# A decoder layer whose planner weighs its streams by a table over time

## The chip, the cores and the metric

One core of one Trainium2 chip runs the kernel. The metric is device time in microseconds (us) of one execution; lower is better. Instruction engines are named as the profile names them: PE (tensor engine; PEld is its weight loads), DVE (vector), ACT (scalar), POOL (GpSimd) and SP (which only issues DMAs here).

## The reference

Four sequences of 1024 rows with 256 features pass one decoder layer. Cut to what matters:

```python
x = x + self_attention(layernorm(x))      # 16 heads of 16; causal; scores mix two products
x = x + cross_attention(layernorm(x), ctx, mask)   # 77 context rows, 16 heads of 16
x = x + ffn(layernorm(x))                 # 256 -> 768 -> 256

# self-attention: Q, K, V = x Wq^T + bq, ...; g = sigmoid(gate), by head
scores = (g * (Q W_cross) K^T + (1 - g) * Q K_mixed^T) / sqrt(16)
out = softmax(causal(scores)) V Wo^T + bo
# feedforward, with int32 weights divided by 127
out = (silu(x Wg^T) * (x Wu^T)) Wd^T
```

All arithmetic is to float32 accuracy.

## The kernel before, in words

**Work and tiles.** The 4096 rows are eight chunks of 512 rows (four sequences, `b`, of two halves, `n`). For each chunk there are five kinds of work. `project` (L975) normalizes the rows and makes keys, queries and values; each key and query block is split into a rounded part `hi` and a rest `lo` (`spread`, L919), which DMAs on SP's queue lay out by heads, since score matmuls use both parts. `maxima` (L1035) computes the scores once and reduces them on DVE to the largest per query (`mt`). `attend` (L1101) computes scores again with keys on the partitions, subtracts the maxima by another matmul (`sel`, `ms`), takes the exponential on ACT (`es`), and multiplies by the values. `cross_attention` (L1254) does the like for the 77 context rows. `ffn` (L1392) has six blocks of 128 hidden features: a gate and an up matmul group of four matmuls each (`wgT`, `wuT`, by `xh` and `xl`), a tanh on ACT (`h`), two products on DVE, then a rounding on ACT and a rest on POOL (`hT`); after two blocks come the down matmuls (`wdT`, `hT`).

**Streams and pieces.** Each kind of work is a stream: a Python generator that yields pieces, `piece(pe, use, at, ...)` (L565). A piece is one stretch of tensor work with the work on other engines that follows it: its estimated PE time, a list of engines with estimated times, the time from which its inputs are there, and the buffers that it takes (PSUM banks as `pair` or `single`, and slots such as `es`, `f2`, `w4`). The streams stand in the order maxima, cross-attention, attention, projection of the first half, projection of the second half, four streams that load weights (one for the cross-attention, three for the feedforward), feedforward. `mode` names how a piece uses the PE array: `rows` (64 rows of it, scores), `cols` (32 columns, values) or `whole`.

**The planner.** `weave` (L645) keeps an account of time while the program is built; nothing of it runs on the chip. At each step it asks for every stream when its next piece could start: inputs there, buffers free, PE free, 0.11 more for a change of mode, and no earlier than its first following engine can take it within a margin. To this time it adds the stream's lateness, `s.lates[s.chunk]` (L669), one number for each stream and chunk from the table `LATES` (L1499). The first stream in order that lies within 0.01 of the smallest sum goes next. The lateness counts in the choice only; the piece is booked at its own time. So a positive number makes a stream yield to others, a negative one puts it ahead. The planner then books PE, engines and buffers, and `perform` (L618) issues the recorded instructions in the order of the planned times, subject to the data they share. Each engine runs its own queue in that order.

**Fillers.** Where the account foresees that PE would idle over 1.3 us (`REST`, L683) while a bank is free, the planner issues matmuls that compute nothing that is used (`selB` by `sel`, `stirred`, L140), (idle - 0.7) / 0.235 of them.

All instructions that the planner issues are recorded under line 643, so the profile tells them apart by tile.

Of the kernel before, what the change touches and what calls it, by code (L numbers as in the profile page):

```python
# [27 lines left out]
def tile_decoder_layer(  # L28
# [68 lines left out]
    class Later:  # L97
        def __init__(self, make, where, steps=()):
            self.make, self.where, self.steps = make, where, steps
# [50 lines left out]
    def single():  # L150
        b = home("single", 8)
        return stirred(banks[:, b, :], banks[:, b, :])
# [163 lines left out]
    for name, sgn in (("cm_qk", 1), ("cm_kq", -1)):  # L316
        t = masks_f[name] = stage.tile([P, P], BF16, name=name + "f")
# [78 lines left out]
    t = single()  # L396
# [3 lines left out]
    for ec in range(NC):  # L400
        t = single()
# [8 lines left out]
    t = single()  # L410
# [10 lines left out]
    t = single()  # L421
# [42 lines left out]
    class Slots:  # L464
# [13 lines left out]
        def give(self, k, when):  # L478
            self.free[k] = when
# [31 lines left out]
    }  # L511
    LATE = 0.2
    SWITCH = 0.11
    WAIT = 0.01

    class Engine:
# [30 lines left out]
    class Stream:  # L547
        def __init__(self, make, lates=()):
            self.lates = lates
            self.chunk = -1  # L550
            self.got = {}
            self.fresh = {}
            self.end = self.done = 0.0
            self.pieces = make(self)
            self.next = next(self.pieces, None)
# [36 lines left out]
    def file(t, spans):  # L592

        last, at = 0, t
        for call in said:
            when = t
            if call[0] != "PE":
                of = [m for m in range(last, len(spans)) if spans[m][0] == call[0]]
                if of:
                    last = of[0]  # L600
                    _, when, at = spans[last]
                else:
                    when = at
            filed.append((when, *call))
        said.clear()
# [39 lines left out]
    def weave(*streams):  # L645
        while True:
            live = [s for s in streams if s.next is not None]
            if not live:
                assert not any(v for s in streams for v in s.fresh.values())
                return  # L650
            can = []
            for s in live:
                p = s.next
                if p["cond"] is not None and not p["cond"]():
                    continue
                t = max(p["at"], *(slots[k].when(c) for k, c in p["take"].items()), 0.0)
                if p["pe"]:

                    if p["mode"] != tensor["mode"]:
                        t = max(t, tensor["end"]) + SWITCH  # L660
                    else:
                        t = max(t + SWITCH, tensor["end"])
                t = max(t, tensor["end"])
                if p["use"] and p["take"]:

                    eng, us = p["use"][0]
                    t = max(t, busy[eng].start(t + p["pe"], us) - p["pe"] - 1.0)
                if t < 1.0e8:
                    can.append((t + (s.lates[s.chunk] if s.lates else 0.0), t, s))  # L669
            assert can, [s.next for s in live]  # L670
            soon = min(c[0] for c in can) + WAIT
            _, t, s = next(c for c in can if c[0] <= soon)
            p = s.next
            s.got = {k: [slots[k].take() for _ in range(c)] for k, c in p["take"].items()}
            for k, tokens in s.got.items():
                s.fresh.setdefault(k, []).extend(i for _, i in tokens)
            s.end = t + p["pe"]
            if p["pe"]:
                idle = t - tensor["end"]
                early = max([slots[k].when(1) for k in ("pair", "single") if k in p["take"]] or [t])  # L680
                if idle > REST and early < tensor["end"] + 0.5 and "selections" in flags:
                    stand["us"] = idle - 0.7
                elif idle > REST:  # L683
                    tensor["slow"] = t + COLD
                s.end += min(max(tensor["slow"] - t, 0.0) / 2, p["pe"])
                tensor.update(end=s.end, mode=p["mode"])
            for token in p["free"]:
                give(token, s.end)
            s.done = s.end
            spans = []  # L690
            for eng, us in p["use"]:
                s.done = busy[eng].run(s.done + LATE, us)
                spans.append((eng, s.done - us, s.done))
            hand["fresh"] = s.fresh
            s.next = next(s.pieces, None)
            hand["fresh"] = None
            file(t, spans)
# [788 lines left out]
    def every(part, lates, chunks=range(NQ)):  # L1486


        def pieces(st):
            for b in range(B):  # L1490
                for n in chunks:
                    st.chunk += 1
                    yield from part(st, b, n)

        return Stream(pieces, lates)
# [8 lines left out]
        [0.1069, 0.1944, 0.3468, 0.0000],  # L1504
        [0.0000, 0.0000, -0.5736, 0.0000, 0.0000, 0.4883, 0.5315, -4.4614],
    )
    streams = [
        every(maxima, LATES[0]), every(cross_attention, LATES[1]), every(attend, LATES[2]),
        *(every(project, LATES[3 + n], [n]) for n in range(NQ)),
        Stream(late_weights), *(Stream(lambda st, m=m: load_ffn(st, m)) for m in range(3)),  # L1510
        every(ffn, LATES[5]),
    ]
    weave(*streams)
    nc = core
    with tc.manual_schedule():
# [6 lines left out]
    t = single()  # L1522
# [53 lines left out]
```

## Time and profile before

| | |
|---|---|
| time, median of 3 runs | 1180.34 us (1180.18 to 1180.37) |
| the profiled execution | 1180.69 us |
| its span in the profile | 1178.1 us |
| mean granted clock of PE | 0.985 |
| DMA | 76.48 MB, 65 GB/s in the mean |
| filler matmuls | 112 |
| maxima's reductions on DVE | 384, 350.9 us |
| exponentials on ACT | 448, 360.2 us |

The span is the time from the first to the last instruction that the profile shows; the rest of the execution's time lies around it. The page gives each engine's busy time and its share of the span, then the chain of work that ended last, then groups of equal instructions: line, engine, operation, output<-input with tile names, shapes, the count, busy time in all, the mean duration of one in ns, and the idle time of the engine just ahead of them with what ended it. A list of waits has the engine and tile that waited, for whom, us in total, times, and the longest. A timeline has start, duration, engine, line, operation, and in brackets the idle time ahead. In a table of stretches each engine has its busy us and in parentheses its instructions; PEclk is the granted share of PE's clock.

### The profile page before, as it was taken

The numbers are of one execution on the slowest core, as the hardware profiler recorded it, in microseconds if no ns is written. First come the engines' busy times: TensorE is split into PE (matmuls) and PEld (weight loads), VectorE is DVE, ScalarE is ACT, GpSimd is POOL, SyncE is SP. The second block draws the span as 40 slices with busy tenths as digits, with TensorE's granted clock in tenths as the row PEclk, the third lists the DMA queues.
The fourth block names the chain that finished last, engine by engine and source line by source line (L and its number), as shares of the span: only waits on it lengthen the run. The fifth ranks groups of instructions, "written<-read, shape, count | busy, mean of one in ns | idle before, by whom it ended". The sixth has DMA issues, their size and how long they took to land.

```text
span 1178.1 us, 22519 instructions
## 1 busy us (share of the span) xinstructions
PE 1108.0 (94%) x9171; PEld 686.8 (58%) x9171; DVE 734.2 (62%) x1287; ACT 558.4 (47%) x785; POOL 131.9 (11%) x138
## 2 busy tenths in 40 slices
PE   5899999999899999999999999999998999999996
PEld 3555545566665565565655557555665555557675
DVE  5578855356588679445668768354689577127444
ACT  3153476554335545744444453675334555862422
POOL 4000100010110010021000011011200000012112
PEclk9799999999899999999999999999999999999999
DMA  6981315639430451125682251034953314004100
GB/s 125 138 133 42 95 27 100 84 57 141 57 72 2 70 72 37 37 33 96 97 119 50 46 70 33 1 99 66 135 83 51 51 25 84 2 1 77 31 36 21
DMA packets 65440, 76.48 MB, mean 65 GB/s; under 512 B 22450, under 2 KB 39398, under 8 KB 65331
## 3 DMA queue, kind: packets, MB, share of 16 engines
q1 hardware_dynamic: 64227, 74.62, 38.8%
q8 instruction: 74, 1.21, 0.5%
q10 hardware_dynamic: 1104, 0.35, 0.1%
q14 instruction: 35, 0.29, 0.1%
HBM read 15.28 MB, written 9.33 MB: 21 GB/s over the span
## 4 chain that ended last, share of the span: by engine, by line
PE 74%; DVE 10%; ACT 6%; DMA 6%; issue 2%; POOL 1%; SPq 1%; ACTq 0%; DVEq 0%; POOLq 0%
PE banks L643 74%; DVE mt L643 5%; ACT es L643 3%; DMA k<-lo 2%; DMA q<-lo 2%; DVE h L643 2%; POOL hT L643 1%; SPq L643 1%; ACT h L643 1%; DMA out_dram<-x 1%; DVE mx L643 1%; ACT hT L643 1%; DMA wk_n<-in_L_attn_Wk_dram 1%; DVE st L643 0%; DVE x L643 0%
## 5 line engine op out<-in xcount | busy, mean ns | idle before, releaser
L643 ACT ACTIVATE es<-banks 128x1024 f32<-128x1024 f32 (+3 forms) x448 | 360.2, 841 | 259.7 <-PE banks L643 235.2
L643 DVE TENSOR_REDUCE mt<-banks 128x2 f32<-128x1024 f32 (+3 forms) x384 | 350.9, 955 | 109.2 <-PE banks L643 105.6
L643 PE MATMUL banks<-k,q 64*128 64x512 f32 (+3 forms) x768 | 160.7, 423 | 17.0 <-DVE mt L643 6.8
L643 PE MATMUL banks<-q,k 64*128 64x512 f32 (+3 forms) x768 | 159.7, 411 | 9.7 <-ACT es L643 3.3
L643 PE MATMUL banks<-es,vs 128*32 128x512 f32 (+3 forms) x1536 | 163.7, 499 | 1.2 <-ACT es L643 0.6
L643 PEld LDWEIGHTS banks<-k,q 64*128 64x128 f32 x768 | 74.4, 187 | 102.3 <-ACT es L643 35.5
L643 PE MATMUL banks<-ms,sel 64*128 64x512 f32 (+3 forms) x768 | 133.6, 343 | 0.1
L643 PEld LDWEIGHTS banks<-q,k 64*128 64x128 f32 x768 | 72.9, 185 | 97.3 <-ACT es L643 50.8
L643 POOL TENSOR_TENSOR hT<-h,hT 128x512 fp32r<-128x512 f32 x48 | 61.6, 1284 | 332.9 <-ACT hT L643 332.9
L643 PEld LDWEIGHTS <-id 64*128 64x128 bf16 x2048 | 61.0, 96 | 51.6 <-issue 38.1
L643 PEld LDWEIGHTS banks<-ms,sel 64*128 64x128 f32 x768 | 73.6, 187 | 3.8 <-DVE ms L643 0.5
L643 DVE SCALAR_TENSOR_TENSOR h<-h,banks 128x512 f32<-128x512 f32 x48 | 33.0, 687 | 65.8 <-ACT h L643 65.2
L643 POOL TENSOR_TENSOR rs<-ve,mhalf 128x4 f32<-128x4 f32 x23 | 24.3, 1059 | 408.7 <-DVE ve L643 408.7
L643 PE MATMUL banks<-cm_qk,id 64*128 64x128 bf16 (+1 forms) x1024 | 68.1, 211 | 0.0
L643 PE MATMUL banks<-cm_kq,id 64*128 64x64 bf16 (+1 forms) x1024 | 66.8, 208 | 0.0
L643 ACT ACTIVATE h<-banks 128x512 f32<-128x512 f32 x48 | 28.7, 597 | 62.6 <-PE banks L643 58.1
L643 PE MATMUL banks<-wdT,hT 128*128 128x256 f32 x384 | 55.6, 294 | 1.3 <-POOL hT L643 0.7
L643 DVE TENSOR_REDUCE mx<-banks 128x8 f32<-128x616 f32 x64 | 47.8, 793 | 12.7 <-PE banks L643 12.7
L643 PEld LDWEIGHTS banks<-es,vs 128*32 128x32 f32 x1536 | 31.8, 108 | 40.8 <-issue 26.1
L643 PEld LDWEIGHTS banks<-wdT,hT 128*128 128x128 f32 x384 | 49.9, 194 | 7.4 <-DVE x L643 1.7
L643 ACT CAST hT<-h 128x512 fp32r<-128x512 f32 x48 | 29.7, 619 | 50.2 <-DVE h L643 50.2
L643 ACT COPY xnT<-banks 128x1024 f32<-128x1024 f32 x31 | 31.3, 1014 | 45.1 <-PE banks L643 45.1
(185 smaller groups left out, 1569.2 us busy)
## 6 DMA issues: line engine op xcount, KB each, us to landing
q<-hi SPq DMA_DIRECT2D x128, 128.0 KB, 5.0
q<-lo SPq DMA_DIRECT2D x128, 128.0 KB, 5.9
k<-hi SPq DMA_DIRECT2D x64, 128.0 KB, 4.8
k<-lo SPq DMA_DIRECT2D x64, 128.0 KB, 5.7
xr<-in_x_dram SPq DMA_DIRECT2D x8, 512.0 KB, 4.7
x<-in_x_dram SPq DMA_DIRECT2D x8, 512.0 KB, 7.1
x_dram<-x SPq DMA_DIRECT2D x8, 512.0 KB, 3.1
out_dram<-x SPq DMA_DIRECT2D x8, 512.0 KB, 2.9
```

The source lines that it names most:

```text
L643: call(*a, **k)
```

## The change

Each stream gets a second table, `nudges`, indexed by the time on the account at which its next piece could start, in stretches of 20 us (`STRETCH`). The number found there is added to the stream's lateness of before. `LATES` stays as it is; so do the streams, their pieces, the estimated times and the buffers. Six streams get a row: maxima, cross-attention, attention, the two projections and the feedforward; the loads of weights have none. The diff, with the table cut to one of its six rows and the start of another:

```diff
     LATE = 0.2
     SWITCH = 0.11
+    STRETCH = 20.0
     WAIT = 0.01
...
         def __init__(self, make, lates=()):
             self.lates = lates
+            self.nudges = ()
...
                 if t < 1.0e8:
-                    can.append((t + (s.lates[s.chunk] if s.lates else 0.0), t, s))
+                    k = int(t / STRETCH)
+                    late = (s.lates[s.chunk] if s.lates else 0.0)
+                    late += s.nudges[k] if k < len(s.nudges) else 0.0
+                    can.append((t + late, t, s))
...
+    NUDGES = (
+        [5.74, -0.22, 0, 0, 0, 0, -0.02, 0.01, 0, 0.09, 0, -0.02, 0, 0,
+         0, 0, 0, -0.03, 0, -0.03, 0, 0, -0.49, 1.97, -1.46, 0, 0, -0.02,
+         0, 0, 0, 0, -0.11, -0.08, 0.09, 0.12, 0, 0.64, 0, 0.02, -0.32, -0.05,
+         0, 0.01, 0.01, 0, 0.16, 0, 0, 1.58, 0, -3.72, 0.20, 0, 0.40, 0.01,
+         3.92],
...
+        [2.94, -1.59, 0.57, -0.01, 0, 0.19, 0.17, -1.10, 2.20, -0.33, -1.81, 0, -0.51, 0.01,
...
+    )
     streams = [
         every(maxima, LATES[0]), every(cross_attention, LATES[1]), every(attend, LATES[2]),
...
         every(ffn, LATES[5]),
     ]
+    for s, row in zip((*streams[:5], streams[9]), NUDGES):
+        s.nudges = row
     weave(*streams)
```

The 341 numbers run from -4.10 to 5.74; 126 of them are 0, and 65 more are below 0.1 in size.

## The prediction, made before the result was known

> **What bounds the kernel now.** I read the page's busy shares first, then its chain of work, then the waits of the tensor engine, and then the stretches where the granted clock drops.
>
> ```profile
> PE 1108.0 (94%) x9171; PEld 686.8 (58%) x9171; DVE 734.2 (62%) x1287; ACT 558.4 (47%) x785; POOL 131.9 (11%) x138
> ...
> PE 74%; DVE 10%; ACT 6%; DMA 6%; issue 2%; POOL 1%; SPq 1%; ACTq 0%; DVEq 0%; POOLq 0%
> ```
>
> The tensor engine (PE) is busy for 1108.0 of 1178.1 us, and 74% of the chain that ends last is its own work. The other engines have room on average. A change of order alone can win only from the 70 us in which PE is idle, from the filler matmuls that the planner puts into idle time it foresees, and from time at a lower clock. Some 15 us of that idle time lies in the start and is not touched. Fillers are one group of the page's longer list:
>
> ```profile
> L643 PE MATMUL banks<-sel,selB 128*128 128x512 f32 x112 | 31.0, 422 | 6.8 <-DVE selB L643 6.6 <-DVE x L643 0.2
> ```
>
> 31.0 us over 112 is 0.277 us each. The waits of PE alone:
>
> ```profile
> PE banks L643 <- ACT es L643: 12.2, 35, 1.8
> PE banks L643 <- DVE mt L643: 11.0, 29, 0.8
> ...
> PE banks L643 <- DVE h L643: 4.5, 4, 1.8
> ```
>
> Most are many and short (0.35 us in the mean); only a few reach 1.8 us, and behind those the clock drops. The same engines by stretches of 5 us (busy time of PE, weight loads, DVE, ACT, POOL, then the granted clock, DMA share and GB/s):
>
> ```profile
> 305.00:310.00 5.00, 3.21 (x28) 1.90 (x26) 1.72 (x3) 1.22 (x2) 2.12 (x2) 1.00 0.09 12
> 310.00:315.00 5.00, 3.22 (x20) 2.98 (x19) 2.71 (x5) 1.92 (x3) 1.68 (x2) 0.56 0.02 5
> 315.00:320.00 5.00, 5.00 (x21) 4.21 (x21) 2.36 (x4) 0.60 (x1) 0.00 (x0) 0.75 0.00 0
> ...
> 672.00:677.00 5.00, 3.14 (x28) 1.25 (x24) 4.73 (x18) 3.45 (x4) 1.02 (x1) 0.89 0.28 76
> 677.00:682.00 5.00, 5.00 (x34) 2.31 (x34) 2.66 (x8) 2.79 (x4) 1.45 (x2) 0.77 0.22 34
> ```
>
> Two waits of 1.79 and 1.78 us stand at 306.7 and 310.0 us. Then the clock is short by 5 x 0.44 + 5 x 0.25 = 3.4 us, some 2.7 us of it while PE works (3.22 x 0.44 + 5.00 x 0.25). That place costs 3.6 + 2.7 = 6.3 us, the dearest after the start. A second lies at 673 us (one wait of 1.86 us), a third at 1092 us (2.19 us, for the query spread's DMAs).
>
> **The change part by part.** Nothing is computed otherwise; every engine but PE issues as many instructions as before, DMAs and their queues included. What changes is which stream's next piece comes first, so I read the built order of both kernels.
>
> *Where the order moves.* In blocks of 20 pieces and more PE's order stays the same over 330 us of the trace (45 to 80, 105 to 210, 334 to 365, 486 to 525, 584 to 683, 768 to 789 us); the start and the end after about 1135 us stay as well. So the 673 us place stays: the DVE order around it, four adds to x with mask work and statistics ahead of the last, is the same row for row. I cost it at 0.
>
> *Fillers.* 112 become 98. The 16 in the start and 57 in the last chunk stay; 39 between become 25. 14 x 0.277 = **-3.9 us**, -3.3 at the 0.235 us that a long run of them is spaced. What hid the waiting was filler; what replaces it is work of other streams that stood elsewhere. If that work now leaves a hole where it came from, up to all of this is given back: the bounds are -3.9 and 0. I take -3.9, since the order shows no filler put in for it.
>
> *Switches of the array's use.* Score matmuls (64 rows), value matmuls (32 columns) and whole-array matmuls alternate. The trace prices a change between them:
>
> ```profile
> 305.15 0.39 PE L643 MATMUL banks<-xh,wgT 128*128 128x512 f32 x1
> ...
> 305.38 0.40 PE L643 MATMUL banks<-xl,wgT 128*128 128x512 f32 x1
> 305.70 0.19 PEld L643 LDWEIGHTS banks<-k,q 64*128 64x128 f32 x2 [0.37 <-issue]
> ```
>
> Starts of the same kind are 0.23 us apart, the change takes 0.32: 0.09 to 0.10 us more. The order has 668 such changes before and 681 after: 13 x 0.1 = **+1.3 us**.
>
> *The place at 306 us.* The first feedforward chunk runs gate, up, gate, up, gate without a break, then 0.6 us of scores, then the third up matmul, which waits 1.79 us:
>
> ```profile
> 302.08 0.60 ACT L643 ACTIVATE h<-banks 128x512 f32<-128x512 f32 x1 [0.32 <-PE banks L643]
> 304.28 0.62 ACT L643 CAST hT<-h 128x512 fp32r<-128x512 f32 x1 [1.60 <-DVE h L643]
> 306.29 0.60 ACT L643 ACTIVATE h<-banks 128x512 f32<-128x512 f32 x1 [1.39 <-POOL hT L643]
> ```
>
> The second tanh waits until POOL has read the first h, so a tanh follows the last by 4.2 us (0.60 on ACT, twice 0.69 on DVE, 0.62 on ACT, 1.28 on POOL, and gaps). From the first tanh (302.08) to the second's product (308.40) it is 6.3 us; PE, with 4.5 us of work in that time, is 1.8 short. In the new order a cross-attention projection (four matmuls of 0.47 us) stands between the second gate and the second up, and 0.75 us of scores behind it. PE then has 0.94 + 0.94 + 1.9 + 0.94 + 0.75 + 0.94 = 6.4 us of work: enough, by 0.1. The POOL waits themselves stay (second to fourth tanh before, second to fifth after; 20 of 48 before, 21 after). Late next is the other wait there, 1.78 us of scores behind ACT, where exps queue behind such a tanh; I keep half of it. The clock dip goes with the long waits: -1.8 - 0.9 - 2.7 = **-5.4 us**, with bounds of -6.3 and 0.
>
> The Trainium skill, "TensorE: Matmul & The Clock Gate" (Part 1: The HAM clock gate), has the clock fall to half after an idle window of about 3.4 us and rise after a busy one. The dips here agree in length (3.4 us short at half speed is 6.8 us, two windows) but not in cause: waits of under 2 us brought them. By the page no dip would belong to these waits, and this term would be -2.7; by the trace it is -5.4.
>
> *Ordinary short waits.* I counted neighbours on PE in both orders: maxima after maxima, where the waits for DVE lie thickest, 131 and 131; attention after maxima 183 and 178; maxima after attention 189 and 191; attention after attention 346 and 352. At a few hundredths to 0.13 us of wait per neighbour that is +0.2 us. Load could still bunch: adding DVE's rows over stretches with 20 us of tensor work each (as the planner counts it), the overrun beyond 20 us is 27 us before and 36 after, but with stretches of 15 us it is 39 and 30. I bound it by -3 and +3 and take **+0.2**.
>
> *New long waits.* The trace has three places of 1.8 us and more outside the start; two lie where the order moves. The new order can make such a place anew, at 1.9 + 1.7 = 3.6 (as at 673 us) to 6.3 us. Taking half a place at the cheaper price gives **+1.8 us**, from 0 to 6.3.
>
> *Sum:* -3.9 + 1.3 - 5.4 + 0.2 + 1.8 = **-6.0 us**. The profiled execution took 1180.69 us, 2.6 outside its span, which stays; so 1174.7, and 0.35 less against the median of the runs (1180.34): **1174.3 us**.
>
> **The rivals.**
>
> *The long wait only moves* (chance 0.14). The POOL waits of tanh are all still there, and the cover I found is 6.4 against 6.3. If PE runs short in that chunk as before, what is left is fillers and switches: -3.3 + 1.3 = -2.0, so 1178.3 us, within what can be told from no change. For it: POOL waits go from 20 to 21. Against it: the projection stands just where the cover lacked.
>
> *A second chain of tanh and POOL* (0.10, slower). In the fifth chunk's feedforward three tanh in a row wait for POOL in the new order, where before two single ones do. The chain of 4.2 us apiece stands against 1.9 us of matmuls; where other streams put less than 2.3 us between, waits add up to 1.8 us and the clock drops: +6.3 us for one such place. It decides from one new place with the old one kept: -3.9 + 1.3 + 6.3 = +3.7, so 1184.0 us. Against it: most runs of POOL waits in the old trace passed without a long PE wait.
>
> *The table does nothing* is excluded: PE's order differs over some two thirds of the time.
>
> **How the numbers follow.** The forecast has 0.76. Its own range is that of its terms: all gains at their ends and 3 us of short waits give -3.9 + 1.3 - 6.3 - 3 = -11.9, so 1168.4; one new place at 6.3 in place of 1.8 gives -1.5, so 1178.8. Reaching into the rivals, and with the sizes unsure, I give 1167.5 to 1181.0. About 0.2% (2.4 us) is what a measurement of this kernel can tell from no change: faster 0.76, within 0.14, slower 0.10.
>
> **What would show it.** Fillers: 98 in the group, 27 us. Switches: gaps of weight loads put down to "issue" up by 1 to 2 us. The 306 us place: no PE wait of 1.8 us for h in the first feedforward chunk (some 15 us earlier in the new order), and the clock at 1.00 there. The place near 673 us returns about 5 us earlier, with its dip. PE's idle total falls to about 67 us, and its busy time by 3 to 5. I am wrong if a new stretch with a clock below 1.00 shows up, or if fillers went and PE's idle time grew by as much.

## The result and the profile after

The changed kernel takes **1171.67 us** (median of 4 runs, 1171.27 to 1173.25) against 1180.34 before: 8.67 us less, a ratio of 0.9921 with a 95% interval of 0.991 to 0.9933. The forecast was 1174.3, the range 1167.5 to 1181.0. The profiled execution took 1171.79 us, its span is 1169.6 us. Three executions that took far longer (1335 us in first400, 3358 in first960, 1989 in before) are left out of the ratios below.

The page of the changed kernel, its busy shares and its chain:

```profile
PE 1103.9 (94%) x9157; PEld 683.9 (58%) x9157; DVE 735.8 (63%) x1287; ACT 559.2 (48%) x785; POOL 132.5 (11%) x138
...
PE 71%; DVE 11%; DMA 7%; ACT 6%; issue 2%; SPq 2%; POOL 1%; ACTq 0%; DVEq 0%; POOLq 0%
```

PE is busy for 4.1 us less and idle for 65.7 us in place of 70.1 (span less busy). Still nothing else bounds the kernel. The fillers, as a group of PE's instructions:

```profile
L645 PE MATMUL banks<-sel,selB 128*128 128x512 f32 x98 | 26.3, 412 | 6.9 <-DVE selB L645 6.9
```

98, with 26.3 us in place of 31.0, as forecast. PE's waits:

```profile
PE banks L645 <- DVE mt L645: 13.2, 28, 1.3
...
PE banks L645 <- ACT es L645: 8.0, 29, 0.6
PE banks L645 <- DVE h L645: 7.2, 6, 2.6
```

Against the same rows of before, the waits for exponentials (`es`) fell by 4.2 us, those for maxima (`mt`) rose by 2.2, and those for the feedforward's `h` rose by 2.7, with a longest of 2.6 us where I had expected the 1.8 us ones to go. The stretches that the prediction showed, in the changed kernel (busy time of PE, weight loads, DVE, ACT, POOL, then clock, DMA share, GB/s):

```profile
305.00:310.00 5.00, 1.86 (x27) 1.28 (x24) 2.98 (x5) 1.93 (x3) 2.06 (x2) 0.97 0.00 0
310.00:315.00 5.00, 5.00 (x24) 4.60 (x24) 1.91 (x3) 0.59 (x1) 0.46 (x1) 0.69 0.00 0
315.00:320.00 5.00, 4.66 (x59) 2.51 (x57) 3.97 (x5) 2.36 (x5) 1.28 (x1) 1.00 0.01 2
672.00:677.00 5.00, 3.16 (x27) 1.70 (x30) 4.76 (x17) 2.63 (x3) 1.02 (x1) 1.00 0.41 131
677.00:682.00 5.00, 5.00 (x42) 1.77 (x34) 4.21 (x13) 4.41 (x6) 1.45 (x2) 1.00 0.21 33
```

The hole at 306 us is still there: PE works for 1.86 of the 5 us from 305 on, and the clock falls behind it (0.97 and 0.69; 5 x 0.03 + 5 x 0.31 = 1.7 us short, before 3.4). The place at 673 us is there too, as costed, but its dip is not: 1.00 in both rows.

**A sum that closes.** To see where 8.5 us of span went, I split PE's time after the first 60 us of each trace into five parts: idle in gaps under 1 us, idle in gaps of 1 us and more, fillers, half of the time that PE works while the trace records the clock at half speed (lost to dips), and the rest. The rest is PE's own work and the end of the span behind PE's last matmul (6.5 to 6.8 us, but 8.1 in zero_1 and 8.0 in zero_2). The rows for the other kernels belong to the experiments below; "account" is how much later the planner's own account of time ends than before's.

| kernel | account | fillers | gaps < 1 us | gaps >= 1 us | filler time | lost to dips | rest | ratio to before, 95% interval |
|---|---|---|---|---|---|---|---|---|
| before | 0 | 112 | 35.8 | 9.9 | 24.9 | 6.2 | 1041.2 | 1 |
| after | -10.8 | 98 | 28.4 | 12.1 | 21.0 | 6.8 | 1041.4 | 0.9921 (0.991 to 0.9933) |
| first400 | -2.9 | 109 | 35.3 | 9.0 | 24.2 | 3.3 | 1044.1 | 0.9992 (0.9982 to 1.0002) |
| first600 | -5.1 | 109 | 33.5 | 10.4 | 24.2 | 6.8 | 1042.7 | 0.9996 (0.9986 to 1.0006) |
| first840 | -1.8 | 127 | 30.8 | 10.5 | 28.3 | 3.4 | 1042.1 | 0.9981 (0.9971 to 0.999) |
| first960 | -7.9 | 103 | 29.8 | 12.8 | 22.4 | 8.5 | 1041.3 | 0.996 (0.9949 to 0.9971) |
| only_max | +14.6 | 118 | 39.9 | 9.2 | 26.3 | 11.2 | 1040.5 | 1.0049 (1.0032 to 1.0066) |
| zero_1 | -7.1 | 100 | 38.3 | 9.4 | 22.0 | 8.1 | 1040.0 | 0.9981 (0.9969 to 0.9992) |
| zero_2 | -5.9 | 101 | 35.3 | 11.5 | 22.4 | 6.3 | 1041.3 | 0.998 (0.9969 to 0.9992) |
| random_1 | +0.4 | 108 | 36.3 | 10.3 | 23.4 | 4.3 | 1043.0 | 1.0015 (0.9999 to 1.0031) |
| more_2 | -11.2 | 98 | 29.2 | 9.7 | 21.0 | 3.4 | 1044.2 | 0.9901 (0.9881 to 0.9922) |
| before_nofill | 0 | 0 | 39.5 | 20.1 | 0 | 15.7 | 1044.9 | 0.9996 (0.9984 to 1.0007) |
| after_nofill | -10.8 | 0 | 29.7 | 24.4 | 0 | 14.7 | 1043.8 | 0.9935 (0.9914 to 0.9955) |
| after_h2 | -10.8 | 98 | 29.8 | 9.3 | 21.0 | 8.3 | 1041.4 | 0.9909 (0.988 to 0.9938) |

Before to after: short gaps -7.4, long gaps +2.2, fillers -3.9, dips +0.6, rest +0.2, in all -8.3 of the span's 8.5 (what is left is rounding). So the forecast's total was about right, and its inside was not: the short gaps, which I had left as they were, gave most of it, and the long waits, on which I had counted, gave nothing. The table rests on one trace for each kernel, the ratio on all runs that were compared. In the later comparisons the same kernel scattered by 2 to 5 us around its median; that dips fall at other places from one execution to the next would do that, but only one execution of each kernel has a trace. "Lost to dips" is worked out, not measured: in first400 and more_2, with 2.9 and 2.8 us less of it than before, the rest is 2.9 and 3.0 us higher, so it is probably charged too high.

Gain and loss along the span, from the ends of equal shares of PE's matmuls (from 60 us on, fillers left out): after is 1.6 us behind before at 590 us, level at 678, then 3.3 ahead at 772, 4.2 at 944, 5.9 at 1031, and 8.4 at the end.

### The profile page after: what moved, and what is told of

It reads as the page before. It is cut to its first block, busy times and chain, and to the rows that moved or that the text cites. A ratio compares the mean times of both kernels' runs of the same rounds, so it can differ in the third digit from the quotient of the medians.

```text
span 1169.6 us, 22481 instructions
## 1 busy us (share of the span) xinstructions
PE 1103.9 (94%) x9157; PEld 683.9 (58%) x9157; DVE 735.8 (63%) x1287; ACT 559.2 (48%) x785; POOL 132.5 (11%) x138
## 4 chain that ended last, share of the span: by engine, by line
PE 71%; DVE 11%; DMA 7%; ACT 6%; issue 2%; SPq 2%; POOL 1%; ACTq 0%; DVEq 0%; POOLq 0%
PE banks L645 70%; DVE mt L645 5%; ACT es L645 3%; DVE h L645 2%; DMA q<-lo 2%; DMA q<-hi 2%; SPq L645 2%; DMA k<-hi 1%; DVE mx L645 1%; ACT h L645 1%; DMA wk_n<-in_L_attn_Wk_dram 1%; ACT hi L645 1%; DMA out_dram<-x 1%; POOL hT L645 1%; ACT hT L645 1%
## 5 line engine op out<-in xcount | busy, mean ns | idle before, releaser
L645 ACT ACTIVATE es<-banks 128x1024 f32<-128x1024 f32 (+4 forms) x448 | 360.6, 841 | 250.2 <-PE banks L645 219.0
L645 PE MATMUL banks<-k,q 64*128 64x512 f32 (+3 forms) x768 | 161.9, 425 | 19.8 <-DVE mt L645 10.7
L645 PEld LDWEIGHTS <-id 64*128 64x128 bf16 x2048 | 62.0, 96 | 51.2 <-issue 38.3
L645 ACT CAST hT<-h 128x512 fp32r<-128x512 f32 x48 | 29.7, 619 | 55.7 <-DVE h L645 55.5
```

The costliest lines, as they stand in the source:

```text
L645: call(*a, **k)
```

## The experiments

Two theories stood at the start. **Theory 1:** the gain is what the planner's account sees, spread over many short waits, so it follows the account's end. **Theory 2**, the reasoning of the prediction: the gain is fillers and a few long waits with their dips; short waits stay.

**The table cut short: first400 and first960.** Up to the cut the account, and so the order, is that of the changed kernel.

```diff
-        s.nudges = row
+        s.nudges = row[:20]
```

> The table is kept for the first 400 us of the planner's account and is 0 behind it, so the order is the new one up to there. Theory 1 (the table's worth is what the planner's account says, in all its stretches, at about 0.8 of it on the chip): the account's end moves by -2.9 us, so -2.3, about 1178.0 us. Theory 2 (the gain sits in few places: long waits with their clock dips, and fillers): in the trace of the new kernel the work that ends this part lies 0.5 us later than before, since a wait for h near 308 us and a clock dip near 112 us took back what was won near 230 us; so 1180 to 1181 us, no gain.

Measured: 0.9992, some 0.9 us less, with 1 in its interval. That is nearer to Theory 2 (no gain) than to Theory 1 (2.3 us).

```diff
-        s.nudges = row
+        s.nudges = row[:48]
```

> The table is kept for the first 960 us of the planner's account and is 0 behind it; fillers 103. Theory 1: the account's end moves by -7.9 us, so -6.3, about 1174 us. Theory 2: in the trace of the new kernel the work of this part ends 2 to 2.5 us earlier than before and the last sixth gives the other 6; with the old lateness in that sixth its two dear things stay (fillers, and the wait of 2.2 us with a dip), so 1177 to 1178.5 us.

Measured: 0.996, about 4.7 us faster. Short gaps fell by 6.0 us, already most of what the whole table takes. The long gaps and dips together are 5.2 us worse than before's, not better. That speaks against Theory 2. The time itself lies between the two: 6.3 us less was Theory 1's figure, 1.8 to 3.3 Theory 2's.

**No fillers: before_nofill and after_nofill.** In both, the planner plans them as before and the order is the same; only the matmuls are not issued.

```diff
     def stirred(t, part):
-        for _ in range(int(stand["us"] / 0.235)):
+        for _ in range(0):
```

> The kernel before with its 112 fillers not issued (order unchanged). Without its fillers the new kernel lost 1.4 to 3 us: 21 us of fillers behind the start went, 13.6 us came back as waits, clock dips went from 6.8 to 13.1 us and matmuls behind them ran slower by 4. If the 14 fillers of difference are worth what they measure (3.9 us) and no more, this kernel is as far from the new one without fillers as the two with fillers are less up to 3.9: 1179 to 1184 us, and the idle time of the tensor engine, free of fillers, still differs by 5 us or more between the two orders. If all of the gain came from the fillers, the two without fillers are within 2 us of each other, 1173 to 1176 us.

> The new kernel with its 98 fillers not issued (planner and order otherwise unchanged). If fillers only stand in idle time, the time stays at 1171.7 within 1 us, except where PE then rests long enough for the clock to drop: up to 5 places at 1.7 us, so 1172 to 1180 us. A gain of more than 1 us would mean that fillers held up work.

Measured: 0.9996 and 0.9935. The two orders stay 0.6% apart without any filler, so most of the gain is not filler time. Taking out 24.9 and 21.0 us of fillers brought 13.9 and 13.6 us of idle time in their place, 9.5 and 7.9 us more lost to dips, and 3.7 and 2.4 us more in the rest. Between the two kernels without fillers the short gaps differ by 9.8 us, more than the 7.4 us by which their spans differ. The page of before without fillers:

```profile
PE 1095.5 (93%) x9059; PEld 672.9 (57%) x9059; DVE 734.1 (62%) x1287; ACT 558.5 (47%) x785; POOL 131.9 (11%) x138
```

PE is busy for 12.5 us less than before, and the span is 2.0 us longer (1180.1 against 1178.1). So the fillers as a whole are not time lost: somewhat over half of their time stands in holes that would be there without them, and the rest is made up for by fewer dips and faster work. "Fewer fillers" is a gain only where the hole goes too, and filler time has to be read together with idle time and dips.

**The place at 306 us: after_h2.** The order is that of the changed kernel; `h` gets two buffers of its own, so that a tanh need not wait for POOL to read the `h` before (the space comes from one `f2` buffer and from two small rings).

```diff
+        own = (pools["h"][1], "h") if name == "h" else (n, kind)
...
-            return pool.tile(shape, dt, tag=kind, name=name, bufs=n)
+            return pool.tile(shape, dt, tag=own[1], name=name, bufs=own[0])
...
-        ("es", 6), ("f2", 6), ("ms", 2), ("mx", 2), ("q", NQ * NC), ("k", NQ * NC), ("v", NQ),
-        ("x", 3),
+        ("es", 6), ("f2", 5), ("ms", 2), ("mx", 2), ("q", NQ * NC), ("k", NQ * NC), ("v", NQ),
+        ("x", 3), ("h", 2),
```

> The new kernel, same order, with the tanh's output h in two buffers of its own beside five shared ones (before: six shared ones, of which several h in a row got the same one); two small rings on DVE are cut from 4 to 2 to make room. If the tanh's wait for POOL makes the waits for h (2.6 us at 308 us, 1.5 at 432, 1.4 at 514, 1.4 at 1143 us) and two of the four clock dips (1.7 each), these go: -6 to -9 us, 1163 to 1166 us. If the waits have another cause, the time stays at 1171.7; if five buffers are too few for the other users, it is later.

In the changed kernel, the chain that makes the hole, in the order of time:

```profile
306.29 0.60 ACT L645 ACTIVATE h<-banks 128x512 f32<-128x512 f32 x1 [1.38 <-POOL hT L645]
306.92 0.69 DVE L645 SCALAR_TENSOR_TENSOR h<-h,banks 128x512 f32<-128x512 f32 x1 [2.67 <-ACT h L645]
307.71 0.69 DVE L645 TENSOR_TENSOR h<-h,banks 128x512 f32<-128x512 f32 x1
...
308.45 0.38 PE L645 MATMUL banks<-k,q 64*128 64x256 f32 x1 [2.62 <-DVE h L645]
```

PE stood still from some 305.8 us on. The tanh waited 1.38 us for POOL; from its start to DVE's second product it takes 2.1 us more (306.29 to 308.40), and only then is a bank free. With `h` apart, the same stretch and the wait of the same kind of matmul:

```profile
305.00:310.00 5.00, 4.10 (x36) 2.89 (x34) 3.39 (x6) 1.91 (x5) 1.28 (x1) 1.00 0.77 100
310.00:315.00 5.00, 4.47 (x25) 4.09 (x23) 2.88 (x4) 0.73 (x2) 1.27 (x1) 0.66 0.00 0
```

```profile
309.42 0.38 PE L646 MATMUL banks<-k,q 64*128 64x256 f32 x1 [0.90 <-DVE h L646]
```

PE's work in 305 to 310 us rises from 1.86 to 4.10 us and this wait falls from 2.62 to 0.90 us, so POOL is what stretched the hole, as the prediction had it. But the dip stayed (0.66 in 310 to 315 us), others came at 86, 113 and 1144 us (8.3 us lost in that trace against 6.8), and the time, 0.9909 with an interval of 0.988 to 0.9938, cannot be told from that of the changed kernel: far less than was expected of it.

**One row of the table: only_max.** Maxima's row alone is applied.

```diff
-        s.nudges = row
+        s.nudges = row if row is NUDGES[0] else ()
```

> Of the table's six rows only that of maxima is kept; the other five streams have their lateness of before. The planner's account ends 14.6 us later than for the kernel before (1159.2 against 1144.6), with 118 fillers against 112. Theory 1 (the chip follows the account's end by about 0.8 of its change, through the many short waits): +9 to +13 us, 1190 to 1194 us on a chip where the kernel before takes 1181. Theory 2 (only fillers and a few long waits with their clock dips count, short waits stay as they are): 6 fillers more are +1.7, and one place more or less is 3 us, so 1179 to 1186 us.

Measured: 1.0049, about 5.8 us slower where the account ends 14.6 us later. The direction is the account's, the size less than half: Theory 1 had 9 to 13 us more, Theory 2 at most some 5. Alone, this row does harm; what it does beside the others was not tried.

**New tables, made by the account alone: zero_1, zero_2, random_1, more_2.** If Theory 1 holds, any table that lets the account end early must gain. Two were searched from an empty table, one is a control with random entries that leave the account's end alone, and one is a search that went on from the tested table. In this last one, 284 of the 348 entries differ, most of them to no effect: its trace differs from that of the changed kernel in some 290 of 9157 matmuls, taken in order by tile and shape, and from before's in some 2000. The edit is always the numbers, here the beginning of maxima's row in the first:

```diff
-        [5.74, -0.22, 0, 0, 0, 0, -0.02, 0.01, 0, 0.09, 0, -0.02, 0, 0,
...
+        [1.17, 0.05, -0.07, 0, 0, 0, 0, -0.01, -0.03, 0, 0.03, 0, 0, 0,
...
```

> Another table of the same form, searched from an empty one by the planner's account alone; the account ends 7.1 us earlier than that of before (1137.46 against 1144.55; the tested change: 10.8 earlier), with 100 fillers instead of 112. Theory 1 (the gain is what the planner's account sees, spread over many waits under 1 us, and reaches the chip at 0.4 to 0.85 of its size): PE's idle time in waits under 1 us falls from 35.8 us (before, from 60 us of the span on) to 30 to 32, and the time by 3 to 6 us. Theory 2 (fillers and a few long waits; waits under 1 us stay): waits under 1 us stay within 1 us of 35.8; the fillers give 12 x 0.277 = 3.3 us, and the rest is whether a long wait or clock dip more or less comes up (1.7 us each).

> A second table searched in the same way from another seed; the account ends 5.9 us earlier than that of before, 101 fillers, about half as many lines of PE's order changed as by the first. Theory 1: waits under 1 us fall to 31 to 33 us, the time by 2.5 to 5 us. Theory 2: waits under 1 us within 1 us of 35.8, the fillers give 11 x 0.277 = 3.0 us, and clock dips more or less at 1.7 us each.

> Control: 90 random entries, kept only where the account's end stayed within 1.5 us of before's (it ends 0.4 us later); PE's order changes in as many lines as with the second searched table; 108 fillers. Theory 1: waits under 1 us 34 to 37 us, time within 2 us of before. Theory 2: waits under 1 us the same too, fillers 4 x 0.277 = 1.1 us less, clock dips at 1.7 us each. If the time here falls as with the searched tables, neither the account nor the fillers explain what those gain; it is then the scatter of orders.

> The tested table with some entries changed by a further search on the account, which ends 0.4 us earlier than that of the tested change (1133.40 against 1133.76); 98 fillers as there. Theory 1: 1171 to 1172, as the tested change or up to 0.3 us better, waits under 1 us near 28. Theory 2: as the tested change, but for clock dips that fall elsewhere, 1168 to 1175. Whether this beats the tested change is below what can be told unless a dip goes.

Measured: zero_1 0.9981 and zero_2 0.998, some 2.2 and 2.4 us faster; random_1 1.0015, with 1 in its interval; more_2 0.9901. Both searched tables fell short of Theory 1, though in time alone their intervals (1 to some 3.7 us faster) still reach its ranges. Their short gaps are 38.3 and 35.3 us where 30 to 32 and 31 to 33 were expected; their gain is about the filler time (2.9 and 2.5 us), as Theory 2 had it, though zero_1's short gaps rose by more than the 1 us that this theory allowed. zero_1 shows what the account does not know: in the first twelfth of its matmuls (from 60 us on), where the account sees hardly any change, its trace has 2.4 us more in gaps and 5.0 more lost to dips; in the third, the place at 306 us is gone, with 3.6 us of long gaps and 2.8 of dips. So **both theories fall**: Theory 2 fails on the tested table, Theory 1 on the two that only the account had chosen. more_2 is the best version of the study (1169.65 us), but its interval and the changed kernel's overlap, so that it is better is not shown.

**Where the short gaps went.** Counting the gaps in twelve equal shares of PE's matmuls (again from 60 us on, without fillers), 6.5 of the 7.4 us by which they fell lie in three: -2.2 in 500 to 591 us, -1.6 in 678 to 772 and -2.8 in 864 to 944; no other share but the first (+1.5) changes by more than 1.0. All three are free of fillers. Stretches of before (columns as above; the first number is PE's busy time):

```profile
500.00:591.00 91.00, 86.69 (x738) 54.90 (x735) 49.80 (x96) 44.05 (x63) 14.28 (x12) 1.00 0.50 76
678.00:772.00 94.00, 91.69 (x742) 55.74 (x742) 58.49 (x98) 51.43 (x68) 9.79 (x9) 0.99 0.28 51
864.00:944.00 80.00, 74.82 (x742) 46.93 (x743) 59.81 (x83) 37.19 (x53) 3.63 (x2) 1.00 0.30 52
```

The same in the changed kernel:

```profile
500.00:591.00 91.00, 88.85 (x756) 55.63 (x754) 51.66 (x103) 46.84 (x66) 15.54 (x13) 1.00 0.46 75
678.00:772.00 94.00, 93.26 (x772) 56.77 (x768) 62.11 (x109) 54.01 (x72) 11.09 (x10) 1.00 0.29 55
864.00:944.00 80.00, 77.63 (x757) 45.94 (x755) 64.51 (x88) 37.87 (x53) 2.38 (x1) 1.00 0.35 52
```

In the same stretches of time PE gets 2.2, 1.6 and 2.8 us more done, and DVE 1.9, 3.6 and 4.7 us more. And in zero_1, which gains little there (zero_2 gains 2.1 us in the third stretch alone, at 76.95):

```profile
500.00:591.00 91.00, 87.10 (x728) 55.14 (x724) 49.80 (x93) 42.97 (x62) 14.27 (x12) 1.00 0.54 84
678.00:772.00 94.00, 91.83 (x756) 55.90 (x756) 57.32 (x101) 52.94 (x69) 8.72 (x7) 1.00 0.26 48
864.00:944.00 80.00, 75.48 (x722) 48.37 (x724) 59.38 (x83) 35.01 (x49) 2.76 (x2) 1.00 0.27 47
```

That gave **Theory 3**: the tested change gains its fillers and the short gaps of these three stretches. Two more cuts of the table test it.

```diff
-        s.nudges = row
+        s.nudges = row[:30]
```

> The tested table cut after 30 stretches (600 us of the account; some 620 us of the span). Account 5.1 us earlier than before's, 109 fillers. By now three theories: Theory 1 (the account's gain arrives at 0.4 to 0.85): 2 to 4.3 us faster, short waits (under 1 us, from 60 us on) 31 to 33.5. Theory 3 (the tested change gains 3.9 us by fillers and 6.5 us of short waits in three stretches of the span, 500 to 591, 678 to 772 and 864 to 944 us, and the account's other gains do not arrive): only the first of the three is in this kernel, so short waits 33 (35.8 less 0.5 as with the first 20 stretches, less 2.2), PE busy in 500 to 591 us up by 2, in 864 to 944 us as in before, fillers 0.8 less, and the time 2 to 4 us less. Theory 2 in its first form (short waits unchanged): 35 to 36.5 and at most 1 us less.

```diff
-        s.nudges = row
+        s.nudges = row[:42]
```

> The tested table cut after 42 stretches (840 us of the account; some 870 us of the span). All three stretches of Theory 3 are ordered much as in the tested change, but the tail is not: the account ends only 1.8 us earlier than before's and plans 127 fillers (15 more than before). Theory 1: 0.7 to 1.5 us faster, short waits 34.5 to 35.3. Theory 3: short waits near 30 (5 to 6 less), PE busy up by about 2, 1.5 and 2.5 in the three stretches; fillers 15 x 0.277 = 4.2 us more; so 0 to 3 us faster, the same as Theory 1 in the time but not in its parts.

first600, whose table ends ahead of the second stretch:

```profile
500.00:591.00 91.00, 88.85 (x756) 55.40 (x750) 51.92 (x104) 46.83 (x67) 15.54 (x13) 1.00 0.46 76
678.00:772.00 94.00, 91.68 (x746) 55.84 (x748) 59.94 (x104) 52.43 (x69) 10.16 (x9) 1.00 0.28 54
864.00:944.00 80.00, 74.82 (x742) 47.03 (x738) 59.79 (x84) 37.46 (x53) 3.64 (x2) 1.00 0.30 51
```

first840:

```profile
500.00:591.00 91.00, 88.86 (x756) 55.74 (x755) 51.77 (x102) 46.03 (x65) 15.52 (x13) 1.00 0.48 76
678.00:772.00 94.00, 93.26 (x774) 56.65 (x768) 62.07 (x108) 54.22 (x72) 10.64 (x10) 1.00 0.29 54
864.00:944.00 80.00, 75.88 (x728) 45.62 (x725) 64.75 (x88) 35.94 (x49) 2.37 (x1) 1.00 0.33 52
```

PE's busy time follows the table stretch by stretch: with its first 30 entries the first stretch has the changed kernel's 88.85 and the others before's 91.68 and 74.82; with 42, the first two have the changed kernel's, and the third is at 75.88, 1.1 of the 2.8 us (some 2.5 were expected). Short gaps are 33.5 us (33 expected) and 30.8 (near 30 expected). The two kernels without fillers differ in the same three stretches by 1.8, 1.6 and 2.9 us, so the gain there does not hang on the fillers. For the place of the gain Theory 3 holds. For the time of first600 it does not: 2 to 4 us were expected and 0.5 came (0.9996; its median lies some 1.5 us below before's), since long gaps (+0.5), dips (+0.6) and the rest (+1.5) took back what short gaps (-2.3) and fillers (-0.7) gave. first840 gained 2.2 us, within what was expected: its 15 added fillers cost 3.4 us, against 5.0 from the short gaps.

Over the kernels with fillers, the sum of idle and filler time goes with the ratios more closely than the account does. It is a part of the time that is to be explained, so this says where the time went and is no forecast. It changed by -9.1 us in after, -10.7 in more_2, -5.6 in first960, -2.1, -2.5 and -1.0 in first400, first600 and first840, -0.9 and -1.4 in zero_1 and zero_2, -0.6 in random_1 and +4.8 in only_max. The times (ratio less 1, times 1181 us) changed by -9.3, -11.7, -4.7, -0.9, -0.5, -2.2, -2.2, -2.4, +1.8 and +5.8: all within 2.4 us of it. The account's ends miss by up to 9. Where fillers are taken out the sum fails: it falls by 11.0 us in before_nofill and 16.5 in after_nofill, and the time by 0.5 and 7.7, because dips and the rest take it back.

## Why the prediction was right, and where it was not

- **Fillers** (-3.9): 98, and -3.9 us of filler time after 60 us. The count is right, and idle time did not rise for it, which the runs without fillers show to be the condition.
- **Switches** (+1.3): the gaps of weight loads put down to "issue" grew by 9.2 us, not by 1 to 2 (129.5 to 137.3 and 43.7 to 45.1), but the rest changed by no more than 0.2 us. No cost of this size is to be seen; it was not tested by itself.
- **The place at 306 us** (-5.4): the rival "the long wait only moves" was right here. The third up matmul no longer waits, but the chain of tanh and POOL caught PE behind the chunk's fifth tanh, where before it was the second and third, with waits of 2.62 and 0.52 us in place of 1.79 and 1.78. In that part of the trace long gaps gave 0.9 and dips 1.2 us: -2.1 in place of -5.4. The failed step is "enough, by 0.1": a cover of 6.4 us against a chain of 6.3, checked for one tanh, where the chain goes on through the chunk at 4.2 us apiece.
- **Ordinary short waits** (+0.2, bounds -3 and +3): -7.4 us, outside the bounds. This is the main error. A mean wait for each kind of neighbour cannot tell an order that puts a maxima piece when DVE is free from one that puts it when DVE is busy: maxima after maxima stood 131 times in both orders, but the gaps under 1 us between two matmuls of maxima add up to 8.0 us before and 6.0 after (from 60 us on). And the count left out the pieces that are neither maxima nor attention: between two of their matmuls these gaps fell from 10.4 to 6.8 us, the largest part. The overrun of DVE's load, 27 to 36 us in blocks of 20 us and 39 to 30 in blocks of 15, had no fixed sign, and I took that for "no change" when it was "not known".
- **New long waits** (+1.8): outside the place at 306 us long gaps cost 3.1 us more and dips 1.7 more (before's dips at 673 and 1092 us, which are gone, already taken off): +4.8.
- **The place at 673 us** (0): it came back with its wait (1.84 us for 1.86), 0.8 us later rather than 5 us earlier, and without its dip.

The parts as measured: -3.9 - 2.1 - 7.4 + 4.8 + 0.1 (rest) = -8.5 us of span. The total was near because +0.2 for -7.4 and -3.6 for +2.7 (the two terms of long waits together) err in opposite directions, by 7.6 and 6.3 us; that was luck. Of the signs named in advance, the fillers came true, PE's idle time fell to 65.7 (about 67 was said), its busy time by 4.1 (3 to 5), and "a new stretch with a clock below 1.00", which was to show the forecast wrong, came three times, while the time still fell.

What stays open is which entries do it in the three stretches; they were not tried one by one. Before's listed waits there are for seven different tiles (`h`, `nat`, `es`, `lo`, `mt`, `mx`, `aS`), each of 0.2 to 2.3 us in a stretch, so no single wait is the cause. The account saw two of these gains about rightly and little of the middle one: its own idle time falls by 2.3, 0.3 and 2.1 us over the same matmuls with the tested table (2.2, 1.6 and 2.8 in the trace). The prediction did not use the account. Read stretch by stretch it might have been the better guide to the short waits, but that is argued and not shown: in zero_1 the account's gain did not arrive.

## What to carry to other kernels

In this kernel, whose bounding engine is 94% busy, the many waits under 1 us were the bulk of what a change of order won. In one like it, compare the engine's busy time over stretches, not the dearest places alone. Count idle and filler time as one sum, look at the dips beside it, and follow a chain of buffer waits to the end of its chunk before calling it covered. A planner's account of time says which order may be better, not by how much: ends of -7.1 and -5.9 us brought 2.2 and 2.4, and -10.8 brought 9.

## What the runs showed of the hardware

Dips of the clock do not belong to a place in the program alone. In the changed kernel there are four of 3.4 us after the start, at 112, 310, 433 and 815 us; three of them:

```profile
108.00:115.00 7.00, 5.16 (x48) 2.67 (x44) 5.55 (x7) 0.68 (x2) 0.00 (x0) 0.77 0.26 92
429.00:436.00 7.00, 5.55 (x33) 3.66 (x32) 5.08 (x6) 2.22 (x5) 2.55 (x2) 0.76 1.08 128
811.00:818.00 7.00, 5.39 (x44) 2.24 (x40) 6.14 (x8) 2.76 (x3) 0.00 (x0) 0.78 1.09 133
```

In each of these stretches PE is idle for only 1.5 to 1.8 of 7 us, and the clock is at half for 3.4 us (7 x 0.23 x 2 = 3.2). At 673 us, on the other hand, a wait of 1.84 us brought no dip, where one of 1.86 us had brought one before. The traces show why. Within each of the fourteen, dips begin and end on one grid of 3.413 us: in before's they begin at 310.6, 675.9 and 1095.7 us, which is 107 and 123 steps apart. I counted PE's busy time in each window of that grid, after 60 us and at full clock. A dip followed all 32 windows in which PE was busy for less than half, 19 of 164 at 0.5 to 0.8, and none of 4258 above. Before's wait at 673 us lies within one window (busy 0.46); in the changed kernel the grid cuts it in two (the lower is 0.62). Thirteen of the traces have this wait, of 1.84 to 1.86 us, and a dip follows it in three. So what counts here is PE's busy share in a window, and where the grid falls decides whether a given wait brings a dip.

Each dip costs some 1.7 us while PE works, if half speed is half the work. That is an estimate and probably high: over the twelve traces with fillers, PE's own work and this charge together rise by only about 0.5 us for each us charged.

The Trainium skill, "TensorE: Matmul & The Clock Gate" (Part 1: The HAM clock gate), describes a free-running window of about 3.4 us, whose phase varies from run to run. That agrees with the grid and the length of the dips, and with their coming and going at the same wait; that a whole idle window is needed, as its table has it, does not agree with windows in which PE was busy for 0.46 to 0.63 here.

Fillers gain by the clock about as much as they cost: without them before's order lost 15.7 us to dips in place of 6.2, and its time was the same (0.9996).
